# Mask and weights loaded by chunks, every second chunk masked on GpSimd, and two output projections moved in among the gates

## Chip, cores and metric

One core of a Trainium2 chip runs the whole program in one launch. The metric is the device time of one execution in microseconds (us). Five engines work side by side, each through its own list of instructions in order: TensorE (PE, matmul), VectorE (DVE), ScalarE (ACT), GpSimd (POOL) and SyncE (SP, which here issues all the DMA transfers). They wait for each other through semaphores.

## What is computed

The input x is 2 x 512 tokens of width 512, all in float32. Four layers are applied, each as x + layer(layernorm(x)):

```
bm  = mask.reshape(16, 32, 16, 32).sum(axis=(1, 3)) > 0      # blocks of 32 x 32
x  += layernorm(x) @ (weight where bm).T + bias              # block-sparse layer
x  += (silu(n @ gate) * (n @ up)) @ down                     # feed-forward, 4-bit weights
proj = n @ in_proj.T                                         # state-space mixer
gate, hBC, dt = split(proj)                                  # 8192, 8192 + 2*1024, 128
x_s, B, C = split(silu(causal_conv(hBC, 4 taps)))            # 128 heads of 64; 8 groups of B and C
y   = scan over chunks of 128 tokens (x_s, B, C, dt) + D * x_s
x  += (rmsnorm(y) * silu(gate)) @ out_proj.T
x  += (silu(n @ gate) * (n @ up)) @ down                     # the same feed-forward again
```

The block mask is given for every element as int32; a block counts when any of its elements is set.

## The kernel before

The tokens stand in 8 tiles of 128. The orders of PE, ACT and DVE are written out by hand in the source, and each of these engines runs its instructions in that order. Those of POOL and SP are put in order by a scheduler when the program is built.

**The block-sparse layer** (`block_sparse`) stands first. SP issues the loads of the tiles 0 and 1 of x, then the whole mask (`mk`, 1 MB), the whole weights (`wt`, 1 MB), tile 2, the bias repeated to 128 partitions, and the tiles 3 to 7. DVE and ACT make the norm of the first two tiles, and PE turns them (L128) into the layout that the matmuls want. DVE sums the mask over rows of 32 in one instruction (L273), a matmul with a block-diagonal matrix of ones (`bd`, L277) sums over the partitions of a block, DVE makes zeros and ones of it (`on`, L279), and four DVE instructions multiply the weights, one for each 128 rows of the width (L283). Then, for each of the 8 tiles, POOL adds the bias to x (L291), four matmuls make the layer's output (`bs_o`, L294), and DVE adds it to x (L305).

**The mixer** (`mixer`) goes through 64 tiles of 128 channels, two at a time: the first pair ahead of the loop, then the phases 1 to 32. In a phase `ph`, three things of different ages stand side by side: the front of the new pair (x channels with their convolution, then the gate), the scan of the pair before, and the output projection of the pair before that. A product of 256 x 512 x 1024 is made by `seven`, a generator with seven steps, which needs seven block products where eight would be usual: each step is four matmul records on PE (the two passes of a float32 matmul are two records) and accumulates in one of three PSUM banks of the tag `proj`. Between the steps the caller places other work. DVE combines the banks (L180, L185, L186, L194, L199).

For x channels and for B and C, the finished bank is convolved: ACT multiplies by the last tap (L551), and three DVE instructions, the taps (L554), add the others, reading the bank. They are kept in a list and issued by `drain`. A bank is free again when its last tap has read it.

The loop of four rounds in the second half of a phase holds the output projections `outs(0)` to `outs(7)`, one for each tile of tokens. Each is two matmuls (L763) into a PSUM bank of the tag `yo`, of which there are three, and a DVE addition into the accumulator (L773, `x_sb` in the profile). Between them stand taps left over from the x front and the products `m * gm` (L718, issued by `flush`). The scan `py` (L729, L738) takes banks of `yo` too, and they are read by L748 when `finish` is called; L748 and L749 make `y` and the new `gt`.

In seven of the phases (`new_group`: 3, 7, ... 27) a new pair of B and C tiles is made after the projections (`group`, seven steps). Then come the matmuls of the scan for the second half of the units, whose banks are read only later, and the gate (`g_front`, again seven steps), which keeps its intermediate results in the buffers `gt` themselves. Each of the four `gt` buffers exists twice, so the new ones take the place of those that the output projections of this phase read. The order there is:

```
                    if ph > 1:
                        next(gate)
                    half_scores(0, c0, heads_new)
                    if ph > 1:
                        next(gate)
                    finish(scans)
                    half_scores(1, c0, heads_new)
```

The output weights `wo` have one buffer; the next load waits until the last projection of the phase has read it.

Of the kernel before, what the change touches and what calls it, by code (L numbers as in the profile page):

```python
# [8 lines left out]
F32 = mybir.dt.float32  # L9
I32 = mybir.dt.int32  # L10
AF = mybir.ActivationFunctionType
ALU = mybir.AluOpType
AX = mybir.AxisListType

P = 128
# [4 lines left out]
DIM = 512  # L20
KC = DIM // P
# [16 lines left out]
def kernel(  # L38
# [25 lines left out]
    nc = tc.nc  # L64
# [5 lines left out]
    psum = ctx.enter_context(tc.tile_pool(name="psum", bufs=2, space=bass.MemoryType.PSUM))  # L70
# [7 lines left out]
    def room(*_):  # L78
        return keep.tile([P, SEQ], F32, tag="tmp", name="tmp", bufs=3)
# [22 lines left out]
    def norm(t):  # L102

        xt = x_sb[:, t, :]
        stats = small.tile([P, 6], F32, name="stats")
        nc.vector.bn_stats(stats, xt)  # L106
        mv = small.tile([P, 2], F32, name="mv")
        nc.vector.bn_aggr(mv, stats)  # L108
        rstd = small.tile([P, 1], F32, name="rstd")
        nc.scalar.activation(rstd, mv[:, 1:2], AF.Sqrt, bias=eps, scale=1.0)  # L110

        def scaled():
            nc.vector.reciprocal(rstd, rstd)  # L113
            xn = room()
            nc.vector.tensor_scalar(xn, xt, mv[:, 0:1], rstd, ALU.subtract, ALU.mult)  # L115
            return t, xn

        return scaled

    def norm_all(t):  # L120
        return norm(t)()

    def turn(normed):

        t, xn = normed
        pt = psum.tile([P, KC, P], F32, tag="tr", name="ln_tr")
        for kc in range(KC):
            nc.tensor.transpose(pt[:, kc, :], xn[:, kc * P : (kc + 1) * P], ident)  # L128
        nc.scalar.copy(xn_t[:, :, t * P : (t + 1) * P], pt)  # L129
# [114 lines left out]
    def block_sparse():  # L244

        with tc.tile_pool(name="bs", bufs=1) as pool:

            def scratch(shape):
                return [pool.tile(shape, ty, name=nm, bufs=2) for nm, ty in (("wi", I32), ("zi", I32), ("sf", F32))]

            wt = pool.tile([P, KC, DIM], F32, name="wt")
            mk = pool.tile([P, KC, DIM], I32, name="mk")
            bias_b = pool.tile([P, DIM], F32, name="bias_b")

            def load_x(t):
                nc.sync.dma_start(x_sb[:, t, :], x_in[t * P : (t + 1) * P, :])

            for t in range(2):
                load_x(t)
            nc.sync.dma_start(mk, mask_t.rearrange("(kc p) n -> p kc n", p=P))  # L260
            nc.sync.dma_start(wt, w_t.rearrange("(kc p) n -> p kc n", p=P))
            load_x(2)
            nc.sync.dma_start(bias_b, bias.to_broadcast([P, DIM]))
            for t in range(3, NT):
                load_x(t)
            normed = [n() for n in [norm(t) for t in range(2)]]
            bd = pool.tile([P, P], F32, name="bd")
            nc.vector.memset(bd, 0.0)
            for i in range(4):
                nc.vector.memset(bd[32 * i : 32 * i + 32, 32 * i : 32 * i + 32], 1.0)  # L270
            NB = KC * DIM // 32
            rows = pool.tile([P, NB], F32, name="rows")
            nc.vector.tensor_reduce(rows, mk.rearrange("p kc (b j) -> p (kc b) j", j=32), AX.X, ALU.add)  # L273
            for n in normed:
                turn(n)
            pb = psum.tile([P, NB], F32, tag="yo", name="pb", bufs=3)
            nc.tensor.matmul(pb, lhsT=bd, rhs=rows, start=True, stop=True)  # L277
            on = pool.tile([P, NB], F32, name="on")
            nc.vector.tensor_scalar(on, pb, 0.0, None, ALU.is_gt)  # L279
            for kc in range(KC):  # L280
                wv = wt[:, kc].rearrange("p (b j) -> p b j", j=32)
                ov = on[:, kc * NB // KC : (kc + 1) * NB // KC]
                nc.vector.tensor_tensor(wv, wv, ov.unsqueeze(2).to_broadcast([P, NB // KC, 32]), ALU.mult)  # L283
            ahead = norm_all(2)
            half = norm(3)
            waiting = []
            half_f = None
            loaded = [dequant_gate(0, scratch), dequant_up(0, scratch)]
            first = []
            for t in range(NT):  # L290
                nc.gpsimd.tensor_add(x_sb[:, t, :], x_sb[:, t, :], bias_b)  # L291
                po = psum.tile([P, DIM], F32, tag="proj", name="bs_o", bufs=3)
                for kc in range(KC):
                    nc.tensor.matmul(  # L294
                        po,
                        lhsT=xn_t[:, kc, t * P : (t + 1) * P],
                        rhs=wt[:, kc, :],
                        start=(kc == 0),
                        stop=(kc == KC - 1),
                    )  # L300
                if t + 2 < NT:
                    turn(ahead)
                if t + 3 < NT:
                    ahead = half()
                nc.vector.tensor_add(x_sb[:, t, :], x_sb[:, t, :], po)  # L305
                if t + 4 < NT:
                    half = norm(t + 4)
                if half_f:
                    waiting.append(half_f())
                half_f = norm(t)  # L310
                if t in (4, 5):
                    first.append(now(loaded.pop(0)))
                if len(waiting) == 2:
                    turn(waiting.pop(0))
            waiting.append(half_f())
        return first, [lambda n=n: turn(n) for n in waiting]
# [99 lines left out]
    def mixer(waiting):  # L416

        with ExitStack() as st:
# [413 lines left out]
            def half_scores(k, c, heads):  # L832

                j, b = units[k // 2]
                if k % 2 == 0:
                    heads[j, b] = []
                    heads["bc"] = load_sums(c + j, b)
                c_t, b_tok, gm = groups[c // CTG][b]
                heads[j, b].append(scores(c + j, b, k % 2, heads["bc"], c_t, gm))
# [6 lines left out]
            for ph in range(1, n_ph + 1):  # L846
                front, last = ph < n_ph, ph >= 2
                c0, c1 = ph * PP, (ph - 1) * PP
                new_group = front and (c0 + PP) % CTG == 0 and ph + 1 < n_ph
# [8 lines left out]
                def finish(scans):  # L858
                    for f in scans:
                        f()  # L860
                    scans.clear()

                def all_squares():
                    for b, y in ys:
                        squares(b, y)
                    ys.clear()
# [12 lines left out]
                def outs(k):  # L879
                    if last:  # L880
                        out_project(ph - 2, [k], gts_old, wo)

                all_squares()
                if last:
                    wo = load_out(ph - 2)
# [34 lines left out]
                both_states(1)  # L920
                finish(half_scan(units[:2]))
                for k in range(4):
                    if front:
                        outs(2 * k)
                    flush()
                    back_scores(4 + k)
                    drain(1 if k < 3 else 0)
                    if made and k in (1, 2):
                        group_scores(made, groups[c0 // CTG], [k - 1])
                    if front:  # L930
                        outs(2 * k + 1)
                    drain(1 if k < 3 else 0)
                flush()
# [25 lines left out]
                if front:  # L959
                    if ph > 1:  # L960
                        next(gate)
                    half_scores(0, c0, heads_new)
                    if ph > 1:
                        next(gate)
                    finish(scans)
                    half_scores(1, c0, heads_new)
                    if ph > 1:
                        next(gate)
                    for u in units:
                        silu(xcs_new[u], xcs_new[u])  # L970
                    next(gate)
                    flush()
                    run(gate)
                    for dst, src in later:
                        silu(dst, src)
                    if made:
                        for b in range(2):
                            for x in made[b]:
                                silu(x, x)
                        groups[(c0 + PP) // CTG] = []  # L980
# [18 lines left out]
            normed = []  # L999
            for t in range(NT):  # L1000
                out_project(n_ph - 1, [t], gts_old, wo_last)
                if t == 2:
                    ms = psum.tile([P, NT], F32, tag="tr", name="ms")
                    for i in range(NT):
                        b, c = divmod(i, NCH)
                        nc.tensor.matmul(
                            ms[:, i : i + 1],
                            lhsT=sq_acc[:, b, c * P : (c + 1) * P],
                            rhs=ones[:, 0:1],
                            start=True,  # L1010
                            stop=True,
# [96 lines left out]
```

## Time and profile before

| | before |
|---|---|
| time, median of 3 runs | 2360.16 us (2359.36 to 2364.12) |
| time of the profiled execution | 2362.27 us |
| its span, first to last instruction | 2360.6 us |
| PE busy | 2302.2 us |
| DVE busy | 1617.0 us |
| ACT busy | 1133.7 us |
| POOL busy | 994.0 us |
| granted TensorE clock, mean | 0.992 |

The profile is of one execution. Its page gives the busy time of each engine, the costliest groups of instructions and the chain of waits. The trace behind it can be asked for more: who waited for whom, the instructions in order of time (timeline), and the busy time of each engine in chosen stretches. In a timeline a row gives the start and the length in us, the engine, the source line, the operation, what it writes and reads, the shape, how many equal instructions stand in a row, and in brackets how long the engine was idle before it and what ended that. PE's records overlap by about 0.16 us[...]; from start to start a full 128x512 record takes 0.43 us.

### The profile page before, as it was taken

How to read it: one execution, taken by the hardware profiler on the slowest of the kernel's cores; microseconds unless marked ns; L12 is line 12 of the kernel's file. 1: busy time of each engine (PE TensorE's matmuls, PEld its weight loads, DVE VectorE, ACT ScalarE, POOL GpSimd, SP SyncE). 2: the span in 40 equal slices, each digit the busy share in tenths (PEclk: the TensorE clock that was granted, in tenths of full speed). 3: DMA queues.
4: the chain of work that ended last, by engine and by line, in shares of the span. 5: the costliest groups of instructions: out<-in, count | busy, mean ns of one | idle time of the engine just before them, and what ended most of it. 6: DMA issues, size and time to landing. Idle time of an engine off the chain costs nothing. (4 is left out here: it accounts for less than half of the span.)

```text
span 2360.6 us, 27338 instructions
## 1 busy us (share of the span) xinstructions
PE 2302.2 (98%) x9626; PEld 1211.0 (51%) x9626; DVE 1617.0 (68%) x2801; ACT 1133.7 (48%) x2430; POOL 994.0 (42%) x963
## 2 busy tenths in 40 slices
PE   8999998999999999999999999999999999879999
PEld 4444444555555555555555555555555555534444
DVE  6454147877778787877878887777778788745520
ACT  2111026556656565666565656556656565521100
POOL 2663023444454444444354444444444453426600
PEclk9999999999999999999999999999999999989999
DMA  5662012222221222122222222222221222236500
GB/s 183 193 203 91 18 40 90 72 72 64 79 80 60 76 79 74 63 72 81 69 66 81 72 66 79 72 72 67 77 81 61 74 80 63 90 114 216 186 14 22
DMA packets 145576, 201.39 MB, mean 85 GB/s; under 512 B 6944, under 2 KB 91808, under 8 KB 145440
## 3 DMA queue, kind: packets, MB, share of 16 engines
q1 hardware_dynamic: 145440, 199.66, 26.6%
q8 instruction: 76, 1.25, 0.2%
q14 instruction: 60, 0.49, 0.1%
HBM read 194.91 MB, written 4.72 MB: 85 GB/s over the span
## 5 line engine op out<-in xcount | busy, mean ns | idle before, releaser
L165 PE MATMUL proj<-xn_t,w 128*128 128x512 f32 x996 | 464.9, 598 | 7.6 <-ACT ce L720 7.0
L721 POOL TENSOR_TENSOR ce<-ce,c_t 128x384 f32<-128x384 f32 x256 | 269.4, 1056 | 457.5 <-ACT ce L720 456.4
L763 PE MATMUL po<-wo,gt 128*128 128x512 f32 x992 | 436.8, 595 | 0.0
L710 ACT ACTIVATE m<-bc,acs 128x128 f32<-128x128 f32 x1024 | 324.6, 389 | 10.3 <-PE py L729 10.3
L165 PE MATMUL proj<-tq,ws 128*128 128x512 f32 x664 | 308.1, 595 | 9.3 <-DVE xc L554 3.7
L763 PEld LDWEIGHTS po<-wo,gt 128*128 128x128 f32 x992 | 184.6, 190 | 219.6 <-issue 194.9
L165 PEld LDWEIGHTS proj<-xn_t,w 128*128 128x128 f32 x996 | 182.2, 191 | 206.6 <-issue 187.8
L718 DVE TENSOR_TENSOR m<-m,gm 128x512 f32<-128x512 f32 x256 | 219.9, 880 | 2.7 <-ACT m L717 2.7
L554 DVE SCALAR_TENSOR_TENSOR xc<-proj,cw,xc 128x511 f32<-128x511 f32 (+2 forms) x288 | 213.5, 742 | 2.5
L658 POOL TENSOR_TENSOR x_dec<-x_dt,dec 128x384 f32<-128x384 f32 x128 | 129.4, 1021 | 181.8 <-DVE x_dt L654 181.2
L165 PEld LDWEIGHTS proj<-tq,ws 128*128 128x128 f32 x664 | 122.1, 190 | 160.6 <-issue 142.6
L151 POOL TENSOR_TENSOR ws<-w 128x256 f32<-128x256 f32 x96 | 72.5, 755 | 307.3 <-DMA w<-in_win_t_dram 292.7
L405 PE MATMUL ffn_o<-down,h_t 128*128 128x512 f32 x448 | 193.4, 592 | 0.0
L729 PE MATMUL py<-m,x_dt 128*64 128x128 f32 x2048 | 183.4, 277 | 3.1 <-DVE m L718 3.1
L773 DVE TENSOR_TENSOR x_sb<-x_sb,po 128x512 f32<-128x512 f32 x248 | 167.8, 678 | 20.6 <-PE po L763 19.6
L756 POOL TENSOR_TENSOR sq_acc<-sq_acc,y 128x512 f32<-128x512 f32 x128 | 177.1, 1398 | 1.4 <-ACT y L755 1.4
L717 ACT ACTIVATE m<-m 128x512 f32<-128x512 f32 x256 | 161.4, 630 | 7.4
L551 ACT ACTIVATE xc<-proj,cb,cw 128x512 f32<-128x512 f32 x96 | 71.1, 775 | 177.4 <-DVE proj L194 156.5
L165 PE MATMUL proj<-tq,w 128*128 128x512 f32 x332 | 156.0, 592 | 0.0
L165 PE MATMUL proj<-xn_t,ws 128*128 128x512 f32 x332 | 156.0, 592 | 0.0
L738 PE MATMUL py<-ce,state 128*64 128x128 f32 x1536 | 151.7, 274 | 0.0
L729 PEld LDWEIGHTS py<-m,x_dt 128*64 128x64 f32 x2048 | 125.3, 138 | 31.1 <-issue 18.2
(164 smaller groups left out, 3257.8 us busy)
## 6 DMA issues: line engine op xcount, KB each, us to landing
bc<-acs_d SPq DMA_DIRECT2D x128, 512.0 KB, 3.7
w<-in_win_t_dram SPq DMA_DIRECT2D x64, 512.0 KB, 3.8
wo<-in_wo_t_dram SPq DMA_DIRECT2D x31, 512.0 KB, 3.7
wi<-in_gate_w_dram SPq DMA_DIRECT2D x14, 512.0 KB, 3.9
zi<-in_gate_z_dram SPq DMA_DIRECT2D x14, 512.0 KB, 5.1
sf<-in_gate_s_dram SPq DMA_DIRECT2D x14, 512.0 KB, 4.7
wi<-in_up_w_dram SPq DMA_DIRECT2D x14, 512.0 KB, 4.6
zi<-in_up_z_dram SPq DMA_DIRECT2D x14, 512.0 KB, 5.7
```

Source lines behind the costliest of these rows:

```text
L165: nc.tensor.matmul(ps, lhsT=a[:, kc, :], rhs=b[:, kc, :], start=(start and kc == 0), stop=(stop and kc == KH - 1), skip_group_check=True,)
L405: nc.tensor.matmul(po, lhsT=h_t[:, fc, t * P : (t + 1) * P], rhs=down[:, fc, :], start=(fc == 0), stop=(fc == NFC - 1),)
L554: nc.vector.scalar_tensor_tensor(dst[:, s:], ps[:, : SEQ - s], cw[:, t, 3 - s : 4 - s], dst[:, s:], ALU.mult, ALU.add)
L710: nc.scalar.activation(m[:, c, :], bc[:, hh, c * P : (c + 1) * P], AF.Relu, bias=acs[:, t, h : h + 1], scale=-1.0,)
L717: nc.scalar.activation(m, m, AF.Exp, scale=-1.0)
L718: mults.append(lambda: nc.vector.tensor_mul(m, m, gm))
L721: nc.gpsimd.tensor_mul(ce, ce, c_t[:, P:].rearrange("p (c l) -> p c l", l=P))
L729: nc.tensor.matmul(py[hh * HD : (hh + 1) * HD, c * P : (c + 1) * P], lhsT=x_dt[:, c, hh, :], rhs=m[:, c, :], start=True, stop=(c == 0),)
L738: nc.tensor.matmul(py[hh * HD : (hh + 1) * HD, c * P : (c + 1) * P], lhsT=state[:, c - 1, hh, :], rhs=ce[:, c - 1, :], start=False, stop=True,
L756: nc.gpsimd.tensor_add(sq_acc[:, b, :], sq_acc[:, b, :], y)
L763: nc.tensor.matmul(po, lhsT=gts[j, b][:, c * P : (c + 1) * P], rhs=wo[:, j, :], start=(j == 0), stop=(j == PP - 1),)
L773: nc.vector.tensor_add(acc[:, t, :], acc[:, t, :], po)
```

## The change

It has two parts. At the start the mask and the weights are loaded in four chunks of 128 rows each, a mask chunk and a weights chunk in turn. The sums over the mask, the small matmuls and the comparison are made chunk by chunk (`count`, `masked`), and the multiplications of the chunks 1 and 3 are given to POOL. The memsets of `bd` move ahead of the norms. In the mixer, in phases that make a new group, the output projections 6 and 7 leave the loop of rounds, and stand after the first and after the second step of the gate.

```diff
-            nc.sync.dma_start(mk, mask_t.rearrange("(kc p) n -> p kc n", p=P))
-            nc.sync.dma_start(wt, w_t.rearrange("(kc p) n -> p kc n", p=P))
+            for kc in range(KC):
+                nc.sync.dma_start(mk[:, kc], mask_t[kc * P : (kc + 1) * P, :])
+                nc.sync.dma_start(wt[:, kc], w_t[kc * P : (kc + 1) * P, :])
...
-            normed = [n() for n in [norm(t) for t in range(2)]]
             bd = pool.tile([P, P], F32, name="bd")
...
-            NB = KC * DIM // 32
-            rows = pool.tile([P, NB], F32, name="rows")
-            nc.vector.tensor_reduce(rows, mk.rearrange("p kc (b j) -> p (kc b) j", j=32), AX.X, ALU.add)
-            for n in normed:
-                turn(n)
-            pb = psum.tile([P, NB], F32, tag="yo", name="pb", bufs=3)
-            nc.tensor.matmul(pb, lhsT=bd, rhs=rows, start=True, stop=True)
-            on = pool.tile([P, NB], F32, name="on")
-            nc.vector.tensor_scalar(on, pb, 0.0, None, ALU.is_gt)
-            for kc in range(KC):
+
+            NB = DIM // 32
+            rows = pool.tile([P, KC, NB], F32, name="rows")
+            on = pool.tile([P, KC, NB], F32, name="on")
+            pb = psum.tile([P, KC, NB], F32, tag="yo", name="pb", bufs=3)
+
+            def count(kc):
+                nc.vector.tensor_reduce(
+                    rows[:, kc], mk[:, kc].rearrange("p (b j) -> p b j", j=32), AX.X, ALU.add
+                )
+                nc.tensor.matmul(pb[:, kc], lhsT=bd, rhs=rows[:, kc], start=True, stop=True)
+
+            def masked(kc):
+                nc.vector.tensor_scalar(on[:, kc], pb[:, kc], 0.0, None, ALU.is_gt)
                 wv = wt[:, kc].rearrange("p (b j) -> p b j", j=32)
-                ov = on[:, kc * NB // KC : (kc + 1) * NB // KC]
-                nc.vector.tensor_tensor(wv, wv, ov.unsqueeze(2).to_broadcast([P, NB // KC, 32]), ALU.mult)
+                eng = nc.gpsimd if kc % 2 else nc.vector
+                eng.tensor_tensor(wv, wv, on[:, kc].unsqueeze(2).to_broadcast([P, NB, 32]), ALU.mult)
+
+            halves = [norm(t) for t in range(2)]
+            count(0)
+            turn(halves[0]())
+            turn(halves[1]())
+            count(1)
+            masked(0)
+            count(2)
+            masked(1)
+            count(3)
+            masked(2)
+            masked(3)
...
+                held = [6, 7] if new_group else []
+
+                def held_outs():
+                    if held:
+                        outs(held.pop(0))
...
                 for k in range(4):
-                    if front:
+                    if front and 2 * k not in held:
                         outs(2 * k)
...
-                    if front:
+                    if front and 2 * k + 1 not in held:
                         outs(2 * k + 1)
...
                     half_scores(0, c0, heads_new)
+                    held_outs()
                     if ph > 1:
                         next(gate)
+                    held_outs()
                     finish(scans)
```

As built, the changed program has on POOL two bias additions (tiles 0 and 1), then the two masks, then the other six bias additions. On SP, in each of the seven phases, the load of the next `wo` stands one load of `w` and one of `bc` later than before. The other orders are those of the source.

## The prediction

> **What bounds the kernel now.** I read the page's first block, then the list of what PE waits for, a table of stretches around one place that the change touches, and the timelines there.
>
> ```profile
> PE 2302.2 (98%) x9626; PEld 1211.0 (51%) x9626; DVE 1617.0 (68%) x2801; ACT 1133.7 (48%) x2430; POOL 994.0 (42%) x963
> ```
>
> PE leads with 98%, but a matmul's record overlaps the next, so only the starts tell of stalls. PE's waits by releaser:
>
> ```profile
> PE proj L165 <- DVE xc L554: 3.7, 8, 1.9
> ...
> PE proj L165 <- DVE c_t L554: 3.6, 7, 0.5
> ...
> PE proj L165 <- DVE b_t L554: 1.9, 7, 0.3
> ```
>
> Seven times each: these are the seven phases in which B and C are made. In all seven the waits are the same (0.27, 0.52 and 0.27 us), so one phase stands for all. The table of stretches gives length, then each engine's busy time in the order PE, PEld, DVE, ACT, POOL:
>
> ```profile
> 504.00:517.20 13.20, 12.93 (x30) 5.45 (x30) 13.03 (x20) 4.56 (x11) 4.92 (x4) 1.00 0.35 110
> ...
> 528.66:542.05 13.39, 12.60 (x30) 5.21 (x29) 11.64 (x16) 10.79 (x23) 3.97 (x5) 1.00 0.12 41
> ```
>
> In the first stretch, the output projections before the group, DVE is busy 13.03 of 13.20 us: it has no more room than PE. PE's timeline of that phase (L763 projections, first L165 rows the group, last three the gate's first steps):
>
> ```profile
> 512.84 1.88 PE L165 MATMUL proj<-xn_t,w 128*128 128x512 f32 x4
> 514.56 1.88 PE L165 MATMUL proj<-tq,ws 128*128 128x512 f32 x4
> 516.70 1.96 PE L165 MATMUL proj<-tq,ws 128*128 128x512 f32 x4 [0.27 <-DVE xc L554]
> ...
> 528.66 1.99 PE L165 MATMUL proj<-xn_t,w 128*128 128x512 f32 x4
> 531.17 1.95 PE L165 MATMUL proj<-tq,ws 128*128 128x512 f32 x4 [0.52 <-DVE c_t L554]
> 533.39 1.95 PE L165 MATMUL proj<-tq,ws 128*128 128x512 f32 x4 [0.27 <-DVE b_t L554]
> ```
>
> and DVE's:
>
> ```profile
> 511.01 0.73 DVE L554 SCALAR_TENSOR_TENSOR xc<-proj,cw,xc 128x509 f32<-128x509 f32 x1
> 511.67 0.67 DVE L773 TENSOR_TENSOR x_sb<-x_sb,po 128x512 f32<-128x512 f32 x1
> 512.26 0.68 DVE L718 TENSOR_TENSOR m<-m,gm 128x512 f32<-128x512 f32 x1
> 513.04 0.69 DVE L773 TENSOR_TENSOR x_sb<-x_sb,po 128x512 f32<-128x512 f32 x1
> 513.65 0.68 DVE L718 TENSOR_TENSOR m<-m,gm 128x512 f32<-128x512 f32 x1
> 514.25 2.31 DVE L554 SCALAR_TENSOR_TENSOR xc<-proj,cw,xc 128x511 f32<-128x511 f32 x3
> ```
>
> The three taps at 514.25 free the proj bank that the group's third step needs: they end at 516.56, and PE starts at 516.70. At the start of the program (timeline):
>
> ```profile
> 12.49 3.57 DVE L283 TENSOR_TENSOR wt<-wt,on 128x512 f32<-128x512 f32 x4
> 13.29 6.45 PE L294 MATMUL bs_o<-wt,xn_t 128*128 128x512 f32 x8 [1.09 <-DVE wt L283]
> 14.21 2.97 POOL L291 TENSOR_TENSOR x_sb<-x_sb,bias_b 128x512 f32<-128x512 f32 x2 [12.23 <-DMA bias_b<-in_bias_dram]
> ```
>
> POOL stands still until the bias lands at 14.04 us; from 20.01 on PE runs without a gap over 0.2 us through the first feed-forward rounds, so what is lost here is lost at the end.
>
> **What the Trainium skill says.** "Perfetto Trace Analysis", Optimization Strategy: the same gap repeating can mean that no buffer is free for the next tile; the trace agrees (0.27, 0.52, 0.27 us in all seven phases, each ended by DVE's last read of a bank). "TensorE: Matmul & The Clock Gate", Part 1: PE runs at half pace until a window of some 3.4 us was busy; the trace agrees (L294's records start 0.86 us apart until 18.54, 0.43 from 19.14 on). "GPSIMD Engine Reference", Engine selection: two-input element work is about 2 times slower there than on VectorE; here 1275 ns (L291) against 687 ns for DVE's 128x512 add. "SBUF — State Buffer", Who interferes with whom: a DVE instruction with two SBUF inputs and a GpSimd one that reads SBUF block each other; L283's last mask took 1.76 us beside L291, the others 0.69.
>
> **The change, part one: projections.** In each of the seven phases projections 6 and 7 (2 x 2 matmuls, 8 records of 0.429 = 3.43 us on PE, two L773 adds on DVE) leave the place before the group and stand after the gate's first and second step. I replay the phase from the rows above; nothing on PE or DVE changes before 509.41 (512.84 - 3.43), where PE is now done with projection 5.
> - Group step 1: 509.41 to 511.13. Step 2 needs a bank that DVE frees with the tap at 511.01, ended at 511.74; with the 0.14 us from DVE's end to PE's start seen above, it starts at 511.88, a wait of 0.75. The first record after a wait takes 0.07 longer (516.70 to 517.21), so it ends at 513.67.
> - DVE now goes from 511.67 through two m products (L718, 0.60 each) to the taps at 512.87, 1.38 earlier than before, ended at 515.18. Step 3 starts at 515.32: a wait of 1.65. So 3.43 us of work left, but the group is only 1.38 earlier. DVE is the cover that is gone: the two projections had hidden its backlog.
> - Everything until the gate's first step keeps this lead: 528.66 becomes 527.28, ended at 529.10. Projection 6 runs 529.10 to 530.82. Step 2's bank is free at 529.65 (taps 528.71 + 2.32 - 1.38), so its old wait (0.68 from start to start, 0.07 for the restart) is covered: 530.82 to 532.54.
> - Projection 7 needs a yo bank; two hold py, whose reads come later, so it takes projection 6's. DVE adds that after the b_t taps, 531.87 to 532.53: projection 7 starts at 532.67, ends 534.46.
> - A new wait: DVE's L180 writes gt[0,1] into the buffer that projection 7's first matmul reads (two buffers each). It starts at 533.80 instead of 533.23; behind it the second add (534.66, when projection 7 has ended) and L748/L749, now 535.26 instead of 533.84. They take 3.46 us as before and end by 538.7, the L185 after them by 539.4, and PE's gate step 6, which waits for it, comes at 539.6: no further stall, with 0.2 us to spare.
> - Gate step 3 starts at 534.46 instead of 533.39: +1.07; its restart (0.07) is gone: +1.0 us. DVE has over 3 us idle at 547.2, so nothing else is late.
> Sum: -1.38 + 3.43 - 0.75 - 0.50 + 0.20 = +1.0; times seven **+7.0 us**. Bounds: +0.7 (wake-ups shorter) to +1.4 (step 6 does wait): +5 to +10.
> SP: the wo load, which waited for projection 7 and was issued at 513.03, now comes after one w and one bc load, at about 535; at 3.7 us it lands near 539, and its first reader is the next phase's projection after 550. Costed at nothing.
>
> **Part two: the start.** Two loads become eight of 256 KB: six more issues of 0.43 to 0.51 us on SP (2.8 us), hidden since the bytes ahead set the landing (mask 9.14, weights 12.28, x 12.94, bias 14.04). DVE's reduce (2.29 us) splits into four that run as chunks land, two masks (0.6 each) leave: DVE is some 2 us earlier. Three more pb matmuls, below the 0.69 us of the one row that is four times as wide, lie in PE's idle time. All this would gain, at most the 0.6 us by which the first L294 could start earlier.
> But in the changed program's order POOL has the first two bias adds ahead of its two masks. They wait for the bias: 14.21, then 2 x 1.27 to 16.75. The masks of chunks 1 and 3 (no row shows this operation on POOL; taken at the bias add's 1.27; 1.0 from the 128x384 row scaled down, 1.71 from the longest row) end at 18.0 and 19.3. So the second matmul of the first tile starts near 18.15, PE having been idle for 4 us and at half pace: two matmuls at 1.71 to 21.6, the last partly warm to 22.8, the next transposes 0.4. The second tile starts near 23.2 instead of 20.01: **+3.2 us**. Bounds: +1.5 (shorter masks, clock back early) to +4.5 (1.71 for each POOL operation). A gain would need the last mask before 18; four POOL operations after 14.04 exclude it.
>
> **Sum.** 7.0 + 3.2 = +10.2 us. The profiled execution took 2362.27 us (2360.6 and 1.7 around it), 2.1 above the median of the three runs: it would become 2372.5, the median **2370.4 us**.
>
> **Rivals.** A, *DVE does not hold the group* (the faster side): if the group's banks came free as PE arrived, all old stalls of a phase would be gone (0.49 at group step 3, 0.75 and 0.50 at the gate: 1.74 us) for the 0.20 at projection 7: 7 x 1.54 = -10.8, with the start's +3.2 some 2352.6. It decides below 1.1 us of stall at group steps 2 and 3 together; I get 2.5, restarts included. For it: the repeated waits are real. Against: DVE busy 13.03 of 13.20.
> B, *only the start or only the phases cost*: break-even in the phases gives 2363; a start that costs nothing gives 2367.
> C, *L180's wait spreads*: L185 late by 0.4 us and gate step 6 with it, 7 x 0.5 more: 2374.
> That the change doesn't do what it says: every second mask does go to POOL, but not before the bias adds.
>
> **Chances.** A measurement of this kernel tells about 0.2% (4.7 us) from no change. My forecast 0.58, C 0.12, B's 2367 0.11, all slower: 0.81; B's 2363, same: 0.11; A 0.08, faster. Range: the forecast's own is 2367 to 2374 (+5 + 1.5 to +10 + 4.5, not both at an end); with C and most of B it is 2364 to 2375.
>
> **What would show it.** In the page after: L165 waits on xc L554 of about 0.6 and 1.5 us, seven times each; the waits on c_t and b_t at the gate gone; a wait of L180 on PE po; the distance between phases with a group (212.3 us over four phases) at 213.3. At the start: bs_o waiting for POOL wt, the first tile ending near 23 us. Wrong if those distances shrink, if POOL masks before the bias, or if the first tile ends before 20 us.

## The result, and the profile after

| | before | after |
|---|---|---|
| time, median of 6 runs each, side by side | 2361.27 us (2359.36 to 2364.12) | 2372.48 us (2368.45 to 2373.02) |
| time of the profiled execution | 2362.27 us | 2368.46 us |
| its span | 2360.6 us | 2366.7 us |

The ratio is 1.0037, with a 95% interval of 1.0026 to 1.0047: the change costs 6.1 to 11.1 us, near 8.7 (2361.27 x 0.0037). The two medians lie 11.2 us apart, at the upper end of that: of the six executions of after two took 2368.5 us and four 2372.3 to 2373.0. The last section shows what goes with such a difference. The forecast was +10.2, as a median of 2370.4 with a range of 2364 to 2375.

The first block of the page after looks like that of before; PE leads again, and nothing in it shows a slower kernel:

```profile
PE 2299.8 (97%) x9632; PEld 1211.3 (51%) x9632; DVE 1612.8 (68%) x2805; ACT 1134.8 (48%) x2430; POOL 996.0 (42%) x965
```

PE is even busy 2.4 us less, in a longer span. What PE waits for tells more (us in total, times, longest):

```profile
PE proj L165 <- DVE xc L570: 14.0, 11, 1.8
...
PE proj L165 <- ACT tmp L177: 2.6, 4, 0.7
...
PE bs_o L310 <- POOL wt L287: 2.1, 1, 2.1
```

The waits on `c_t` and `b_t` at the gate are gone, those on the taps of `xc` (now L570) have grown from 3.7 to 14.0 us, and a wait for POOL's masks is new. PE's timeline of one of the seven phases, first the group's steps 1 to 3, then the gate's steps 1 to 3 with the two moved projections (L779) among them, and its steps 4 to 6:

```profile
724.88 1.88 PE L165 MATMUL proj<-xn_t,w 128*128 128x512 f32 x4
727.41 1.95 PE L165 MATMUL proj<-tq,ws 128*128 128x512 f32 x4 [0.65 <-ACT tmp L177]
730.84 1.96 PE L165 MATMUL proj<-tq,ws 128*128 128x512 f32 x4 [1.48 <-DVE xc L570]
...
742.80 1.98 PE L165 MATMUL proj<-xn_t,w 128*128 128x512 f32 x4
744.62 1.88 PE L779 MATMUL po<-wo,gt 128*128 128x512 f32 x4
746.34 1.88 PE L165 MATMUL proj<-tq,ws 128*128 128x512 f32 x4
748.05 1.96 PE L779 MATMUL po<-wo,gt 128*128 128x512 f32 x4
749.85 1.88 PE L165 MATMUL proj<-tq,ws 128*128 128x512 f32 x4
751.57 3.60 PE L165 MATMUL proj<-xn_t,w 128*128 128x512 f32 x8
755.00 1.88 PE L165 MATMUL proj<-tq,w 128*128 128x512 f32 x4
```

The group now has two stalls, 0.65 and 1.48 us, where it had one of 0.27. The gate has none in brackets. DVE's timeline of the same phase, first what stands ahead of the group's banks, then L180 at the gate:

```profile
726.53 0.73 DVE L570 SCALAR_TENSOR_TENSOR xc<-proj,cw,xc 128x509 f32<-128x509 f32 x1
727.19 1.28 DVE L734 TENSOR_TENSOR m<-m,gm 128x512 f32<-128x512 f32 x2
728.39 2.31 DVE L570 SCALAR_TENSOR_TENSOR xc<-proj,cw,xc 128x511 f32<-128x511 f32 x3
...
749.26 0.69 DVE L180 TENSOR_TENSOR gt<-gt,proj 128x512 f32<-128x512 f32 x1 [1.29 <-PE po L779]
```

The tap at 726.53 ends at 727.26, and step 2 starts 0.15 later. The three taps at 728.39 end at 730.70, and step 3 starts 0.14 later. Between the two, DVE makes two products `m * gm`: step 3 stands behind these. In four of the seven phases the profile names ACT's L177 as the releaser of step 2. L177 ended at 727.39 here, only 0.02 before PE's start, while the two releases by DVE just read took 0.14 and 0.15; experiment e6 below settles that it isn't L177.

The table of stretches (length, then busy time of PE, PEld, DVE, ACT, POOL; then PE's clock and DMA) shows the same around the group:

```profile
718.10:731.30 13.20, 11.08 (x26) 4.50 (x25) 13.12 (x20) 5.96 (x15) 5.90 (x5) 1.00 0.23 79
742.00:756.50 14.50, 14.50 (x48) 6.73 (x45) 12.27 (x18) 11.05 (x22) 4.88 (x6) 1.00 0.21 73
```

In the first, before and into the group, DVE works 13.12 of 13.20 us and PE only 11.08. In the second, the gate, PE has no gap left. The work was moved from a place where DVE was the limit to one where PE was waiting a little, and more was lost at the first than won at the second. From the group's first step to the gate's first step PE takes 17.92 us (742.80 - 724.88) instead of 15.82 (528.66 - 512.84), 2.1 more. The gate's waits that are gone were worth 1.2: from its first to its third step it took 4.73 us before, and 3.62 after when the 3.43 of the two projections are left out; the rest is a restart of 0.08.

At the start, POOL and PE by the timeline:

```profile
13.26 2.94 POOL L307 TENSOR_TENSOR x_sb<-x_sb,bias_b 128x512 f32<-128x512 f32 x2 [11.27 <-DMA bias_b<-in_bias_dram]
16.15 2.23 POOL L287 TENSOR_TENSOR wt<-wt,on 128x512 f32<-128x512 f32 x2
```

```profile
13.14 2.05 PE L310 MATMUL bs_o<-wt,xn_t 128*128 128x512 f32 x2
17.25 4.77 PE L310 MATMUL bs_o<-wt,xn_t 128*128 128x512 f32 x6 [2.06 <-POOL wt L287]
```

POOL's two masks stand behind two bias additions, which wait for the bias. PE's first tile is cut in two, with a pause of 2.06 us between.

**Three marks** of the trace serve for all that follows. The first is the start of the first `pg` matmul (the feed-forward network): 48.86 us before, 51.15 after, +2.3 for the start. The second is the distance of the phases: from ACT's first activation of `c_t` in one group to that in the next, four phases later; there are six such distances, and I take their median. It was 212.26 us before and 213.19 after, +0.93. The third is the time itself. The marks give 2.3 + 7 x 0.93 = 8.8 us, which agrees with the ratio. The profiled span grew by 6.1 only; the last section shows why single executions differ by such an amount.

### The profile page after: what moved, and what is told of

The parts are those of the page before. It is cut to its first block, busy times and chain, and to the rows that moved or that the text cites. A ratio compares the mean times of both kernels' runs of the same rounds, so it can differ in the third digit from the quotient of the medians.

```text
span 2366.7 us, 27361 instructions
## 1 busy us (share of the span) xinstructions
PE 2299.8 (97%) x9632; PEld 1211.3 (51%) x9632; DVE 1612.8 (68%) x2805; ACT 1134.8 (48%) x2430; POOL 996.0 (42%) x965
## 5 line engine op out<-in xcount | busy, mean ns | idle before, releaser
L779 PE MATMUL po<-wo,gt 128*128 128x512 f32 x992 | 439.7, 596 | 0.0
L779 PEld LDWEIGHTS po<-wo,gt 128*128 128x128 f32 x992 | 184.0, 190 | 220.8 <-issue 194.0
L570 DVE SCALAR_TENSOR_TENSOR xc<-proj,cw,xc 128x511 f32<-128x511 f32 (+2 forms) x288 | 213.4, 741 | 2.5
```

Of the source, the lines that this page charges most:

```text
L570: nc.vector.scalar_tensor_tensor(dst[:, s:], ps[:, : SEQ - s], cw[:, t, 3 - s : 4 - s], dst[:, s:], ALU.mult, ALU.add)
L779: nc.tensor.matmul(po, lhsT=gts[j, b][:, c * P : (c + 1) * P], rhs=wo[:, j, :], start=(j == 0), stop=(j == PP - 1),)
```

## The experiments

Ten kernels ran. The times of each are compared with those of before on the same chip.

| | edit | median us | ratio, 95% interval | first pg | distance |
|---|---|---|---|---|---|
| before | | 2361.3 to 2363.1 | 1 | 48.86 | 212.26 |
| after | | 2372.48 | 1.0037 (1.0026 to 1.0047) | 51.15 | 213.19 |
| e1 | start alone | 2364.31 | 1.0008 (1.0000 to 1.0016) | 50.71 | 212.55 |
| e2 | phases alone | 2367.84 | 1.0021 (1.0012 to 1.0030) | 49.13 | 213.06 |
| e3 | start, all masks on DVE | 2363.47 | 1.0003 (0.9994 to 1.0011) | 48.88 | 212.54 |
| e4 | start, two bias additions on DVE | 2362.63 | 1.0002 (0.9994 to 1.0010) | 46.85 | 212.25 |
| e5 | phases, taps first | 2359.70 | 0.9986 (0.9979 to 0.9992) | 48.87 | 211.88 |
| e6 | phases, one projection | 2359.81 | 0.9987 (0.9981 to 0.9994) | 47.99 | 211.82 |
| e7 | taps first alone | 2359.39 | 0.9984 (0.9978 to 0.9991) | 49.34 | 211.75 |
| e8 | one projection, taps first | 2352.10 | 0.9953 (0.9939 to 0.9966) | 48.75 | 210.82 |
| e9 | e8 with the start of e4 | 2350.95 | 0.9948 (0.9934 to 0.9961) | 48.26 | 210.70 |
| e10 | e8 again | 2352.39 | 0.9956 (0.9943 to 0.9968) | 48.51 | 210.70 |

Two things limit the marks. Seven executions have the start of before (before, e2, e5 to e8, e10), and their first `pg` lies between 47.99 and 49.34, as the first transfers land earlier or later: a difference of up to 1.35 us between two single profiles says nothing of the start. And some distances are longer than the others of their profile by 0.2 to 0.75 us. In e1 and e3 four of the six are, which lifts their medians (the least of the six is 212.24 and 212.25 there, 212.26 before). Most of this extra time arises at one place, the `py` matmuls some 107 us after the mark in before, e1, e3 and e4, which follow DVE's last product `m * gm`. Why it comes in some phases and not in others stays open.

### e1 and e2: each part alone

e1 is the kernel after without the projections' move, e2 the kernel before with it.

```diff
 e1, from after
-                held = [6, 7] if new_group else []
...
-                    if front and 2 * k not in held:
+                    if front:
...
-                    held_outs()
```

> The start as changed, the mixer as before. My theory (the two masks on POOL stand behind two bias adds, which wait for the bias): the first feed-forward matmul (pg) starts at 51.2 us as in the changed kernel, 2.3 later than before's 48.86, and the phases with a group repeat every 212.3 us as before; in all +2.3 us. Rival (the whole loss is in the phases, the start costs nothing): pg near 48.9 and no change in time. The executions of one kernel differ by up to 4 us, so pg's start and the repeat distance decide, not the median.

> The start as before, projections 6 and 7 among the gates as changed. My theory (DVE holds the proj banks of the group's second and third step, so leaving out two projections there only uncovers its backlog): pg at 48.9, the phases with a group repeat every 213.2 us (+0.95), two new waits of 0.65 and 1.48 us in each, in all +6.7 us. Rival (the loss is all in the start, the moved projections cover the gate's waits): repeat at 212.3 or below, no loss.

e1 is slower by 0.0 to 3.8 us by its interval, near 1.9; the first `pg` comes 1.85 later. e2 is slower by 2.8 to 7.1, near 5.0, with a distance of +0.8 (7 x 0.8 = 5.6). Both parts cost, and 1.9 + 5.0 = 6.9 agrees with the 6.1 to 11.1 of the whole within the intervals. The stall of each part stays with it. PE in e1, at the start:

```profile
17.00 4.58 PE L310 MATMUL bs_o<-wt,xn_t 128*128 128x512 f32 x6 [2.02 <-POOL wt L287]
```

and in e2, at the group:

```profile
727.94 1.96 PE L165 MATMUL proj<-tq,ws 128*128 128x512 f32 x4 [0.64 <-ACT tmp L177]
731.37 1.96 PE L165 MATMUL proj<-tq,ws 128*128 128x512 f32 x4 [1.47 <-DVE xc L554]
```

So both parts cost, and rival B falls. For e1 the time alone is at the edge of what can be told; its mark (1.4 us above the latest of the seven starts of before) and its stall carry the verdict.

### e3 and e4: what is slow at the start

Both have the mixer of before and the start of after. e3 gives all masks to DVE; e4 leaves two with POOL and gives the first two bias additions to DVE.

```diff
 e3
-                eng = nc.gpsimd if kc % 2 else nc.vector
+                eng = nc.vector
 e4
-                nc.gpsimd.tensor_add(x_sb[:, t, :], x_sb[:, t, :], bias_b)
+                badd = nc.vector if t < 2 else nc.gpsimd
+                badd.tensor_add(x_sb[:, t, :], x_sb[:, t, :], bias_b)
```

> The changed start, but all four masks on DVE; the mixer as before. My theory (the loss is POOL's queue): the wait of the first tile on POOL is gone. DVE's two further masks (0.6 us each) put the last small matmul and so the first bs_o about 0.6 later, near 13.8; from there the tile takes 6.45 us at half pace as before, and pg starts near 49.4, 0.5 later than before and 1.7 earlier than with the changed start. Rival (the chunks themselves, eight loads and four small matmuls, cost the time): pg stays at 51.

> The changed start, masks of chunks 1 and 3 on POOL, but the bias adds of tiles 0 and 1 given to DVE, so that nothing stands ahead of the masks on POOL; the mixer as before. My theory: mask 1 starts on POOL right after its comparison (near 12.1) and mask 3 near 15.2, ended by 16.4, before PE asks for it at half pace (13.14 + 3 x 1.71 = 18.3); the first tile is whole in one go and pg starts near 48.7, 2.4 earlier than with the changed start. Rival (masks on POOL are slow in themselves, or block DVE): pg at 50 or later.

POOL and PE in e4:

```profile
11.67 1.05 POOL L287 TENSOR_TENSOR wt<-wt,on 128x512 f32<-128x512 f32 x1 [9.68 <-DVE on L284]
13.94 1.05 POOL L287 TENSOR_TENSOR wt<-wt,on 128x512 f32<-128x512 f32 x1 [1.22 <-DVE on L284]
```

```profile
12.68 5.05 PE L311 MATMUL bs_o<-wt,xn_t 128*128 128x512 f32 x8
```

With the bias additions out of POOL's way, the same masks on the same engine run as soon as `on` is there, and PE does its first tile in one piece. So it is not POOL's pace that costs at the start of the changed kernel, but its order: the masks stood behind additions that waited for the bias. The first `pg` comes at 46.85, further ahead than I expected (48.7), and outside the range of the seven starts; e3's 48.88 is a little ahead of the 49.4 expected, and inside it. Nor do the eight loads and the small matmuls cost the time, which was e3's rival: both kernels keep them. That the loss is gone rests on the mark and on the stall. In time e3 and e4 are the same as before, but their intervals overlap e1's too. The 2.0 us that e4's profile is ahead at `pg` can't be seen in its times. In that profile they are gone by the second group mark, where e4 stands at 522.89 and before at 521.86; the section on the hardware shows what took them.

### e5, e6 and e7: is it DVE's order that holds the group?

All three have the start of before. e5 has the mixer of after and one call more, e6 holds only projection 7, e7 is before with that call alone.

```diff
 e5 and e7
                 for k in range(4):
+                    if new_group and k == 3:
+                        drain()
 e6
-                held = [6, 7] if new_group else []
+                held = [7] if new_group else []
```

What `drain()` issues is the list of taps. It puts the last taps of the x front ahead of the last round's products `m * gm` and of its projection adds. The expectations below say that gate work is drained ahead of the taps; it is the taps that go first.

> Start as before, mixer as after (projections 6 and 7 held into the group), but VectorE's queued gate work is drained ahead of the taps of group step 3, so that the taps no longer stand behind gate multiplies. Theory (the new waits come from VectorE being late with the taps that hold the projection banks): the wait at group step 3 falls from 1.5 us to about 0.45, that at step 2 stays at 0.65 to 0.75; distance between phases with a group about 212.1 instead of 213.1 (before: 212.3), seven times, so about 1.4 us under before and 8 under the mixer of after alone. Rival (the stalls are not made by VectorE's order but by the group coming too early for any order): distance stays at 213.1 to 213.2, about 5 to 6 us over before. One execution of any kernel scatters by some 4 us, so the distance of the phases decides and the time only confirms.

> Start as before, mixer as after, but only projection 7 is held and stands among the gates; projection 6 runs where it ran before. Theory: the group then comes about 0.7 instead of 1.4 us too early for VectorE, group step 2 has no wait, step 3 one of about 1.35, and the gate waits are still covered by the one projection; distance 211.9 (before 212.3, after 213.2), about 2.4 us under before. Rival (one held projection does not cover the gate waits): the gate waits on c_t and b_t come back with 0.4 us or more and the distance is 212.4 or higher, no gain.

> The kernel before with one edit: VectorE's queued gate work is drained ahead of the taps of group step 3; no projection is moved. Theory: the old wait at group step 3 (0.27 us shown, 0.49 start to start) goes, distance about 211.8 instead of 212.3, seven times: 3.4 us under before. Rival (the drained gate work was needed earlier or later by something else, so the wait only moves): distance stays within 0.1 of 212.3, no change.

DVE and PE in e5, at the group:

```profile
723.35 2.96 DVE L554 SCALAR_TENSOR_TENSOR xc<-proj,cw,xc 128x509 f32<-128x509 f32 x4
726.23 1.28 DVE L718 TENSOR_TENSOR m<-m,gm 128x512 f32<-128x512 f32 x2
```

```profile
724.23 1.96 PE L165 MATMUL proj<-tq,ws 128*128 128x512 f32 x4 [0.52 <-DVE xc L554]
726.46 1.95 PE L165 MATMUL proj<-tq,ws 128*128 128x512 f32 x4 [0.27 <-DVE xc L554]
```

The same work in another order: the two products (1.28 us) now come after the taps, and the wait at step 3 falls from 1.47 to 0.27. Step 2 still waits 0.52. The distance falls from 213.06 (e2) to 211.88, further than the expected 212.1, and the time from 5.0 us over before to 3.3 under it. The rival of e5, that the group simply came too early for any order, falls.

PE in e6, the group's steps 2 and 3:

```profile
726.64 1.88 PE L165 MATMUL proj<-tq,ws 128*128 128x512 f32 x4
729.65 1.96 PE L165 MATMUL proj<-tq,ws 128*128 128x512 f32 x4 [1.13 <-DVE xc L554]
```

and ACT:

```profile
726.84 0.59 ACT L177 COPY tmp<-proj 128x512 f32<-128x512 f32 x1 [5.10 <-PE proj L165]
```

With one projection more ahead of the group, step 2 has no wait and step 3 one of 1.13 (expected 1.35). ACT's L177 stands behind step 1 here as in the kernel after, and it runs from 726.84, when step 2 has already begun. So step 2 doesn't need it, and its releaser in the kernel after was the tap. One projection among the gates is enough to cover both gate waits: in e6's list of PE's waits `c_t` and `b_t` are missing.

e7 moves no work between the places, and gains 0.5 in the distance (0.49 expected) and 3.8 us in time. The old wait at step 3 is gone, the gate waits are what they were; PE's waits by releaser:

```profile
PE proj L165 <- DVE c_t L554: 3.6, 7, 0.5
...
PE proj L165 <- DVE xc L554: 2.2, 1, 2.2
PE proj L165 <- DVE b_t L554: 1.9, 7, 0.3
```

The one wait of 2.2 left on `xc` stands at 421 us, in the first group, ahead of the seven phases. e5 isn't better than e7 (211.88 against 211.75, and 3.3 against 3.8 us under before): with the taps first, moving both projections wins nothing more.

### e8, e9 and e10: a version that beats both

```diff
 e8, from before
+                held = [7] if new_group else []
...
+                    if new_group and k == 3:
+                        drain()
...
+                    held_outs()
```

> Start as before; only projection 7 stands among the gates, and the gate work is drained ahead of the taps of group step 3. Theory: neither the group steps nor the gates wait; distance 210.6 to 210.9 instead of 212.3, seven times: 10 to 12 us under before. Rival (the removed stalls appear later, at group step 4 or where the gate multiply holds its buffer): distance 211.5 or higher, under 6 us gained.

PE in e8, from the group to the gate, and the stretch from 722.12 to 754.11 in the table of stretches:

```profile
722.12 1.88 PE L165 MATMUL proj<-xn_t,w 128*128 128x512 f32 x4
723.84 3.60 PE L165 MATMUL proj<-tq,ws 128*128 128x512 f32 x8
...
737.68 1.98 PE L165 MATMUL proj<-xn_t,w 128*128 128x512 f32 x4
739.50 1.88 PE L763 MATMUL po<-wo,gt 128*128 128x512 f32 x4
741.22 3.60 PE L165 MATMUL proj<-tq,ws 128*128 128x512 f32 x8
```

```profile
722.12:754.11 31.99, 31.99 (x129) 15.86 (x128) 25.71 (x38) 15.33 (x30) 6.23 (x8) 1.00 0.21 67
```

Steps 2 and 3 stand in one row of eight, at the group and at the gate: PE has no gap over 32 us. The distance is 1.44 shorter than before, seven times 10.1 us, and the times say 11.1 (8.0 to 14.4). The two edits together bring more than one by one (0.44 in e6 and 0.51 in e7), because each takes away the stall that the other leaves: e6's step 3, e7's gate.

> Both parts mended: at the start chunks with every second mask on GpSimd, the first two bias additions on VectorE (as in e4); in the phases only projection 7 held and the gate work drained before the taps (as in e8). Theory: the first pg at 46.9 (2.0 earlier than before), distance of the phases 210.8 as in e8, so the marks from the second group on are some 2 us earlier than in e8 and the time is 2348 to 2352, unless the half-speed windows of the clock around 350 to 415 us take the 2 us back as they did in e4. Rival (the start's 2 us are always lost in the windows): the same as e8, 2352.

> The kernel of e8 once more, beside e9 on the same chip: 2352, distance 210.8, first pg near 48.8; it tells whether e9's start is worth anything beyond e8.

e9 and e10 ran side by side: 2350.95 (2348.25 to 2353.98) and 2352.39 (2348.86 to 2354.47), five runs each. The mended start isn't worth anything that these runs can tell. In e9's profile the first `pg` came at 48.26, not 46.9 as expected: the chunks landed 0.7 to 1.0 us later than in e4, and POOL's first mask began at 12.70 instead of 11.67. So whether a start that is 2 us ahead would last to the end isn't settled.

## Why the prediction was right, point by point

- **DVE is the cover that is gone**: shown. Predicted were waits of 0.75 and 1.65 at the group's steps 2 and 3, from start to start, and of about 0.6 and 1.5 in the profile's brackets. Measured are 0.81 (727.41 - 724.88 less the 1.72 of a step) and 1.64 (730.84 - 727.41 less the 1.79 of a step that starts after a wait), and 0.65 and 1.48 in brackets. Compared with e2, e5 changes nothing but DVE's order and brings step 3 from 1.47 to 0.27; e6 changes nothing but the amount moved, which takes away step 2's wait and leaves 1.13 at step 3; e8, with both, has neither.
- **The gate waits are covered**: they are gone from the list, and e6 shows that one projection would have covered them.
- **L180's new wait without harm to PE**: L180 starts 6.46 us after the gate's first step (predicted 6.52), with a wait on `po`, and the gate's step 6 follows without a stall. Rival C falls. That it is the `gt` buffer that holds L180 rests on the source and this timeline alone; no run changes it. Projection 7 was to wait 0.20 for its bank and didn't: it starts 1.71 after the gate's second step.
- **The load of `wo`**, costed at nothing: SP issued it at 750.34 us in the phase shown, 7.5 after the gate's first step (7.7 predicted), and no wait of PE on it appears.
- **+1.0 us per phase**: from the group's first step to the gate's third it is 24.97 us in the phase shown (749.85 - 724.88), and 20.55 in before (533.39 - 512.84); less the 3.43 of the two projections that is +0.99, where +1.07 was predicted; the restart that is gone takes it to +0.91 (+1.0 predicted). The distances say +0.93, and +0.8 in e2. The term of +7.0 measured 6.5 in the marks and 2.8 to 7.1 in the times of e2.
- **Part two, +3.2 at the start**: this term was too large; it measured +2.3 at the first `pg`. The mechanism held, POOL's masks behind bias additions. PE's second matmul was put at 18.15 and came at 17.25, after a pause of 2.06 where 4 us were assumed. The step that failed is that everything else at the start would keep its time: the bias additions began at 13.26, not at 14.21, with the loads that they wait for (13.00 to 13.31 in the three profiles that have the chunks and this order on POOL, 13.99 to 14.28 in the seven with whole loads). That is -0.95. The prediction had taken it that the bytes ahead alone set the landing; in eight loads the last weights landed at 11.27 instead of 12.28, and the bias at 13.09 instead of 14.04. From the first addition to the first mask took 2.89 instead of twice 1.27, +0.35: the second addition took 1.71, and the row of before that the prediction shows has 2.97 for the same two. From that mask's start to PE's took 1.10 instead of 1.40, -0.30. These two errors nearly cancel, which is luck.
- **The mask on POOL**, taken at 1.27 us from the bias addition, takes 1.05, and 1.23 for the second one in after and e1. "GPSIMD Engine Reference", Engine selection, in the Trainium skill calls two-input work about 2 times slower than on VectorE; the mask is 1.5 times (1.05 against 0.69), and 1.8 times where it took 1.23. For the first mask, the one that PE waits for, the bound of 1.0 from the 128x384 row was the better price.
- **Rival A** asked for less than 1.1 us of stall at steps 2 and 3; there were 2.13 in brackets, and 2.5 from start to start, as predicted. It described a DVE that isn't late; e8, which makes DVE less late by its order and by moving less, has lost the stalls that the rival wanted gone. That its 2352.10 is so near the rival's 2352.6 is chance: the rival's number holds +3.2 for a start that e8 doesn't have.
- **The sum**: +10.2 predicted, +8.8 by the marks, with 0.9 of the difference in the start and 0.5 in the phases. The times allow 6.1 to 11.1, so they don't tell 10.2 and 8.8 apart.

## What to carry to other kernels

Work that is moved off a place can be the cover of another engine's backlog there: before moving it, look at what the other engine still has to do between the freed place and the next buffer, and in which order. Moving half as much, or putting the instruction that frees the buffer ahead of those that free nothing, can turn the same idea from a loss into a gain: here from +5.0 to -3.1 and -3.3 us, each alone, and to -11.1 with both. The order alone, with nothing moved, gave -3.8. On an engine whose order a scheduler decides, read the built order: two short instructions behind one that waits for a late load wait as long as that one does.

## What the runs showed of the hardware

I had not expected that executions of one and the same kernel lie over 6 us apart (before: 2358.93 to 2365.37 over 57 runs) and that the granted clock goes with it. The mean granted clock of these 57 was 0.991 in 33 (median 2363.96 us), 0.992 in 18 (2362.34) and 0.993 in six (2359.79). So too with the six of after: the two at 2368.5 had 0.993, the four at 2372.3 and more 0.991. The profiles show where the clock differs. e8 and e10 are the same program. The table of stretches, first e8, then e10, for the beginning of the mixer, where PE has pauses:

```profile
340.00:420.00 80.00, 62.55 (x241) 32.50 (x239) 63.17 (x99) 43.20 (x92) 30.66 (x31) 0.94 0.24 79
```

```profile
340.00:420.00 80.00, 64.24 (x236) 32.95 (x234) 61.30 (x97) 43.28 (x92) 29.82 (x31) 0.89 0.25 79
```

PE's mean clock was 0.94 in one and 0.89 in the other: the clock record has 10.2 us at half speed between 300 and 450 us in e8, 17.1 in e10. From the first matmul into `pd`, at the end of the feed-forward part (320.06 and 319.82), to the second group mark (520.02 and 522.44) e8 took 199.96 us and e10 202.62: 2.7 us for 6.8 us more at half speed. Near 2070 us it is the other way round: 27.3 us at half speed in e8 and 20.5 in e10, and e10 takes 1.7 us less from the second feed-forward's first `pg` to the end (284.11 against 285.83). The stretches at half speed last 3.413 us or a multiple of it. "TensorE: Matmul & The Clock Gate", Part 1, in the Trainium skill says that the window runs free of the kernel's start; this agrees with two executions of one program getting different windows. The twelve profiles agree with it further. In each PE stands still from 26.0 to 30.0 us after its first matmul into `pd`. In the five with 10.2 us (before, after, e1, e5, e8) the half speed begins 29.43 to 29.93 us after that matmul, in the seven with 17.1 us 28.35 to 29.21. So the time at half speed goes with where the windows fall on PE's pause. That the one causes the other isn't shown: no run moves them against each other on purpose.

This also answers where e4's 2.0 us went and why the profiled span of after grew by 6.1 only. e4's profile has 17.1 us at half speed at the mixer's start, before's has 10.2: from `pd` to the second group mark e4 took 204.73 and before 201.69. In the profile of after, the stretch near 2070 has 20.5 us at half speed where before's has 27.3, and from the second feed-forward's first `pg` to the end it took 283.78 us instead of 285.79: 2.0 of 8.2 us were given back there, in this execution.
